# An attention block between two int8 feed-forward blocks on one core: score steps regrouped into nine full-PSUM cycles, with a new hand-placed order

## Chip, core and metric

The kernel runs on one core of a Trainium2 chip. The metric is the device time of one execution in microseconds; 2193.93 us is the median of three runs before the change (2192.86 to 2195.85). Five engines work side by side, each through its own list of instructions in the order in which the program issues them: TensorE (PE in the profile, its weight loads PEld), VectorE (DVE), ScalarE (ACT), GpSimd (POOL) and SyncE (SP), which here issues every DMA. TensorE writes only to PSUM, which has eight banks of 128 partitions by 512 float32; a result must be read out by ScalarE or VectorE before its bank can be written again.

## The reference, cut to what matters

```python
def ffn(lhs, rhs):                                   # int8 feed-forward, rhs 512x512
    lhs_scale = max(absmax(lhs, axis=2), 1e-12) / 127
    rhs_scale = max(absmax(rhs, axis=0), 1e-12) / 127
    acc = int8(round(lhs / lhs_scale)) @ int8(round(rhs / rhs_scale))
    return acc * lhs_scale * rhs_scale

def attn(x, Wk, Wq, Wv, Wo, bo, ...):                # 16 heads of 32
    k, q, v = x @ Wk.T, x @ Wq.T, x @ Wv.T
    k, q = layernorm_per_head(k, kln_g, kln_b), layernorm_per_head(q, qln_g, qln_b)
    dot = causal(einsum('bihd,bjhd->bhij', q * s, k * s))
    return einsum('bhij,bjhd->bihd', softmax(dot), v) @ Wo.T + bo

x = x + 0.5 * ffn(layernorm(x), rhs)                 # x is (8, 1024, 512) float32
x = x + attn(layernorm(x), ...)
x = x + 0.5 * ffn(layernorm(x), rhs)
```

## The kernel before

**Units.** There are 8 batches of 1024 tokens and 16 heads. The work is cut into 32 units; a unit is one batch and a group of four heads (`Unit`, L1220). Tokens go in tiles of 128, eight to a batch. All matrix products of the attention are float32; the two feed-forward products are bf16.

**What a unit does.** For each token tile `project` (L1231 to L1240) makes q, k and v of the four heads: four products over the 512 inputs, 384 columns wide, in two halves. `take` copies them out of PSUM on ScalarE (a square, a copy of q and k, a copy of v). `squares`, `logs`, `newton` and `divide` normalise q and k over a pair of tiles; `block`, `send` and `fetch` transpose them through DRAM; `gain` applies the learned scale. Then the scores are made twice. `m_scores` (L1367) makes them with queries on the partitions, and `m_max` (L1386 and L1392) reduces them on VectorE to each query's negative maximum; `m_both`, `m_turn` and `m_wide` (L1405 to L1423) send it through DRAM so that `m_shift` (L1435) subtracts it from q. `e_scores` (L1447) then makes the shifted scores with keys on the partitions, `e_exp` (L1467) takes the exponential on ScalarE into a tile `pt`, GpSimd zeroes the part above the diagonal (L1471) and adds `pt` tiles up for the denominators (`e_add`, L1488). `e_sum` (L1498) multiplies `pt` with v into `p_o`; `e_out` copies it out; `e_den` (L1516), `e_fold`, `e_rec`, `e_wide` and `e_mult` turn the sums of `pt` into reciprocals and multiply.

**Tiling of TensorE.** A score product has only 32 rows (one head), so four of them run at once in the four row groups of the array: rows of the profile marked 32*128. `e_sum` and `e_den` have 32 columns per head and run four at once in column groups (128*32). Everything else uses the whole array (128*128).

**Steps.** A unit has nine score tiles of 512 columns for the maxima (`MTILES`) and nine for the exponentials (`ETILES`), each for two pairs of heads. `fill` (L1579) issues one tile of one head pair of each kind: four heads side by side. So a unit has 18 steps. The pair of heads that runs in the maximum differs from the one in the exponential, and the two kinds are of neighbouring units, shifted by two steps.

**PSUM before.** `ps_m` and `ps_e` are two banks each, one buffer each: every step writes both, and the next step can't start until `m_max` and `e_exp` have read them. `ps_p` (two buffers of a bank) serves `project` and the output product, `ps_x` (one bank) the feed-forward products, `e_den` and transposes, and `p_o` (one bank) is open over the ten sums of `SUMS`, three for the first half of the queries and seven for the second.

**Feed-forward and output.** `First` (L1110) does the first feed-forward of one token tile and the layer norm ahead of the attention; `Last` (L1169) multiplies a token tile's attention output with Wo (`project`, L1184 and L1186, four products and a bias), adds x and does the second feed-forward. Each unit carries two tiles of each. `Norm` (L996) takes statistics on VectorE, makes `ve`, `rstd` and `off` on GpSimd and applies them on ScalarE. The attention output stays in SBUF (`oT`, ten buffers of 128x512).

**Order.** No scheduler runs: every piece of work has a place, a number in steps, in one of the tables `PLACES` (for units 0 to 29), `BEGIN` and `END`. The pieces are sorted by unit times 18 plus place, and issued in that order; that is the order on every engine and of the DMAs on SP. Waits come from the data alone.

Of the kernel before, what the change touches and what calls it, by code (L numbers as in the profile page):

```python
# [15 lines left out]
P = 128  # L16
# [8 lines left out]
STEPS = 18  # L25
ROWS = 12
COLS = 6
SKEW = 2

# [14 lines left out]
SUMS = [(0, [0]), (1, [0, 1]), (2, [0]), (3, [0]), (2, [1]), (4, [0]), (5, [0]), (6, [0]), (7, [0])]  # L44
SUMS.append((8, [0, 1]))
FIRST_SUMS = (0, 3)
LAST_SUMS = (2, 9)
# [12 lines left out]


PLACES = {
    ('sum', 0): 5.76,
    ('add', 0, 0): 16.945,
    ('add', 0, 1): -44.756,
    ('sum', 1): 8.25,
    ('add', 1, 0): 6.75,
    ('add', 1, 1): 8.69,
    ('sum', 2): 8.4,
    ('add', 2, 0): 8.114,  # L70
    ('add', 2, 1): 10.315,
    ('sum', 3): 11.425,
    ('add', 3, 0): 25.206,
    ('add', 3, 1): -4.272,
    ('sum', 4): 11.495,
    ('add', 4, 0): 12.483,
    ('add', 4, 1): 11.717,
    ('sum', 5): 12.804,
    ('add', 5, 0): 12.935,
    ('add', 5, 1): 12.5,  # L80
    ('sum', 6): 18.244,
    ('add', 6, 0): 15.9,
    ('add', 6, 1): 13.525,
    ('sum', 7): 18.31,
    ('add', 7, 0): 17.065,
    ('add', 7, 1): 15.19,
    ('sum', 8): 18.465,
    ('add', 8, 0): 20.55,
    ('add', 8, 1): 18.625,
    ('sum', 9): 19.911,  # L90
    ('add', 9, 0): 20.96,
    ('add', 9, 1): 21.25,
    ('out', 0): 10.283,
    ('out', 1): 20.235,
    ('den', 0): 12.75,
    ('fold', 0): 13.375,
    ('rec', 0): 18.5,
    ('wide', 0): 19.625,
    ('mult', 0): 23.125,
    ('den', 1): 23.38,  # L100
    ('fold', 1): 24.636,
    ('rec', 1): 26.25,
    ('wide', 1): 26.489,
    ('mult', 1): 29.251,
    ('m', 'both'): 17.25,
    ('m', 'wide'): 18.19,
    ('m', 'turn'): 17.81,
    ('shift', 0): 19.451,
    ('shift', 1): 22.71,
    ('project', 0, 0): 1.5,  # L110
    ('project', 0, 1): 1.911,
    ('take', 0): 2.424,
    ('project', 1, 0): 2.288,
    ('project', 1, 1): 2.625,
    ('take', 1): 2.636,
    ('project', 2, 0): 3.625,
    ('project', 2, 1): 4.125,
    ('take', 2): 5.05,
    ('project', 3, 0): 4.375,
    ('project', 3, 1): 6.375,  # L120
    ('take', 3): 7.125,
    ('project', 4, 0): 7.935,
    ('project', 4, 1): 9.255,
    ('take', 4): 9.625,
    ('project', 5, 0): 9.81,
    ('project', 5, 1): 10.56,
    ('take', 5): 12.25,
    ('project', 6, 0): 13.425,
    ('project', 6, 1): 14.875,
    ('take', 6): 15.875,  # L130
    ('project', 7, 0): 15.864,
    ('project', 7, 1): 16.25,
    ('take', 7): 16.44,
    ('squares', 0): 3.756,
    ('logs', 0): 3.786,
    ('divide', 0): 6.25,
    ('squares', 1): 7.315,
    ('logs', 1): 8.27,
    ('divide', 1): 10.69,
    ('squares', 2): 12.668,  # L140
    ('logs', 2): 13.25,
    ('divide', 2): 15.739,
    ('squares', 3): 17.864,
    ('logs', 3): 18.636,
    ('divide', 3): 19.853,
    ('block', 0): 6.625,
    ('block', 1): 12.19,
    ('block', 2): 16.745,
    ('block', 3): 19.96,
    ('first', 0): {'load': -7.904, 'begin': -4.565, 'root': 1.125, 'norm': 3.114, 'scale': 4.489, 'round': 6.06, 'whole': 7.9, 'flip': 8.201, 'product': 10.429, 'add': 10.5, 'store': 11.125, 'root2': 13.31, 'norm2': 18.375, 'block': 18.5, 'send': 22.25},  # L150
    ('last', 0): {'load': 6.125, 'low': 7.125, 'high': 7.25, 'begin': 7.765, 'root': 8.5, 'norm': 9.0, 'scale': 9.685, 'round': 11.625, 'whole': 11.9, 'flip': 11.972, 'product': 16.065, 'add': 17.865, 'store': 30.9},
    ('first', 1): {'load': -25.875, 'begin': 7.375, 'root': 8.272, 'norm': 11.75, 'scale': 14.86, 'round': 16.38, 'whole': 18.494, 'flip': 19.9, 'product': 21.125, 'add': 22.625, 'store': 24.62, 'root2': 25.076, 'norm2': 26.625, 'block': 27.125, 'send': 29.125},
    ('last', 1): {'load': 15.05, 'low': 17.625, 'high': 19.3, 'begin': 19.375, 'root': 19.386, 'norm': 20.011, 'scale': 20.96, 'round': 22.185, 'whole': 23.69, 'flip': 24.054, 'product': 26.75, 'add': 27.25, 'store': 52.125},
    ('newton', 0): 4.96,
    ('newton', 1): 9.424,
    ('newton', 2): 13.375,
    ('newton', 3): 19.05,
    ('send', 0): 8.199,
    ('fetch', 0): 8.701,
    ('gain', 0): 10.815,  # L160
    ('send', 1): 12.549,
    ('fetch', 1): 15.875,
    ('gain', 1): 17.75,
    ('send', 2): 17.646,
    ('fetch', 2): 18.315,
    ('gain', 2): 19.9,
    ('send', 3): 20.25,
    ('fetch', 3): 20.565,
    ('gain', 3): 24.136,
    ('bring', 0): -4.825,  # L170
    ('bring', 1): -2.81,
    ('bring', 2): -0.386,
# [629 lines left out]
def macaron_kernel(  # L802
# [179 lines left out]
    def rhs_row(c):  # L982
# [3 lines left out]
        if c == NK - 1:  # L986
            nc.vector.tensor_copy(rs_bc, p_rs)
# [815 lines left out]
```

## Time and profile before

| | |
|---|---|
| median of three runs | 2193.93 us |
| span of the profiled execution | 2191.2 us |
| VectorE, ScalarE, GpSimd busy | 1722.6, 1380.5, 1816.7 us |
| instructions | 40293 |
| DMA | 268.01 MB, 49.7% of 16 engines' span |
| `p_qkv` products (L1240) | 709.4 us in 1920 records |
| score products, 512 columns (L1367, L1447) | 434.6 and 430.1 us in 1536 records each |
| adds of `pt` on GpSimd (L1488) | 1071.6 us in 620 |
| exponentials of 1024 columns (L1467) | 586.9 us in 576, mean 1020 ns |
| maxima of 1024 columns (L1386) | 312.5 us in 256, mean 1221 ns |

A float32 product appears as two records, so 1920 records of `p_qkv` are 960 products. A record's duration contains the time in which it overlaps its neighbours, so on TensorE the distance between starts says more than the durations. `nmT` (L1412) is written once in a unit and marks the units: 25 of them start between 429.9 and 1961.5 us, which is 63.82 us for each; the five between 183.9 and 429.9 us, which carry no second feed-forward yet, are 61.5 us apart.

### The profile page before, as it was taken

How to read it: one execution, taken by the hardware profiler on the slowest of the kernel's cores; microseconds unless marked ns; L12 is line 12 of the kernel's file. 1: busy time of each engine (PE TensorE's matmuls, PEld its weight loads, DVE VectorE, ACT ScalarE, POOL GpSimd, SP SyncE). 2: the span in 40 equal slices, each digit the busy share in tenths (PEclk: the TensorE clock that was granted, in tenths of full speed). 3: DMA queues.
4: the chain of work that ended last, by engine and by line, in shares of the span. 5: the costliest groups of instructions: out<-in, count | busy, mean ns of one | idle time of the engine just before them, and what ended most of it. 6: DMA issues, size and time to landing. Idle time of an engine off the chain costs nothing. (4 is left out here: it accounts for less than half of the span.)

```text
span 2191.2 us, 40293 instructions
## 1 busy us (share of the span) xinstructions
PE 2089.8 (95%) x12881; PEld 927.6 (42%) x13000; DVE 1722.6 (79%) x4029; ACT 1380.5 (63%) x2719; POOL 1816.7 (83%) x2376
## 2 busy tenths in 40 slices
PE   5899999999999999999999999999999999999887
PEld 2444443444444444444444444444444444444332
DVE  7677777888888888888878888888888877776776
ACT  5556666666666666666666666666666666556454
POOL 5348898888999898899889889888989888887665
PEclk9999999999999999999999999999999999999998
DMA  6234554555555555555555555555555554443221
GB/s 192 68 104 117 119 126 119 129 132 118 128 134 133 142 138 139 120 130 133 131 141 143 135 121 130 133 132 141 143 137 114 125 126 110 122 113 87 64 60 64
DMA packets 715318, 268.01 MB, mean 122 GB/s; under 512 B 472673, under 2 KB 669281, under 8 KB 715106
## 3 DMA queue, kind: packets, MB, share of 16 engines
q1 hardware_dynamic: 715106, 265.43, 49.7%
q8 instruction: 103, 1.69, 0.3%
q14 instruction: 109, 0.89, 0.1%
HBM read 166.22 MB, written 82.82 MB: 114 GB/s over the span
## 5 line engine op out<-in xcount | busy, mean ns | idle before, releaser
L1488 POOL TENSOR_TENSOR pt<-pt,pt 128x768 f32<-128x768 f32 (+1 forms) x620 | 1071.6, 1736 | 52.2 <-PE p_o L1498 25.1
L1467 ACT ACTIVATE pt<-p_t 128x1024 f32<-128x1024 f32 x576 | 586.9, 1020 | 523.3 <-PE p_t L1447 485.6
L1240 PE MATMUL p_qkv<-wall,yT 128*128 128x384 f32 x1920 | 709.4, 500 | 0.0
L1367 PE MATMUL p_s<-qk 32*128 32x512 f32 (+3 forms) x3072 | 657.3, 523 | 32.3 <-DVE nm L1392 22.3
L1392 DVE CUSTOM_DVE_ANT_0 p_s<-p_s,masks 128x128 f32<-128x128 f32 (+3 forms) x1024 | 511.1, 499 | 223.9 <-PE p_t L1447 171.9
L1447 PE MATMUL p_t<-qk 32*128 32x512 f32 (+3 forms) x3072 | 647.1, 524 | 6.2 <-DVE qk L1435 4.5
L1240 PEld LDWEIGHTS p_qkv<-wall,yT 128*128 128x128 f32 x1920 | 343.4, 189 | 310.6 <-issue 122.0
L1386 DVE TENSOR_REDUCE nm<-p_s 128x2 f32<-128x1024 f32 x256 | 312.5, 1221 | 118.2 <-PE p_t L1447 107.1
L1367 PEld LDWEIGHTS p_s<-qk 32*128 32x128 f32 x3072 | 228.7, 184 | 379.1 <-issue 189.4
L1471 POOL TENSOR_SCALAR_AFFINE_SELECT pt<-pt 128x256 f32<-128x256 f32 x512 | 230.2, 471 | 107.3 <-ACT pt L1467 103.8
L1498 PE MATMUL p_o<-pt,v 128*32 128x512 f32 (+3 forms) x3072 | 293.4, 497 | 1.1 <-ACT oU L1509 1.1
L1447 PEld LDWEIGHTS p_t<-qk 32*128 32x128 f32 x3072 | 245.2, 185 | 49.1 <-issue 10.8
L1186 PE MATMUL p_w_b<-wo,oT 128*128 128x512 f32 x496 | 231.0, 598 | 4.5 <-issue 4.5
L1350 ACT ACTIVATE qk<-qk,qk_b,qk_g 128x256 f32<-128x256 f32 x240 | 130.2, 591 | 108.8 <-DMA qk<-qkd 108.8
L1498 PEld LDWEIGHTS p_o<-pt,v 128*32 128x32 f32 x3072 | 86.8, 110 | 193.6 <-issue 141.4
L1392 DVE DVE_READ_ACCUMULATOR2_ANT nm<- 128x1 f32 x1024 | 144.6, 141 | 0.0
L1186 PEld LDWEIGHTS p_w_b<-wo,oT 128*128 128x128 f32 x496 | 92.5, 191 | 82.2 <-issue 76.6
L1257 ACT ACTIVATE sq<-p_qkv 128x256 f32<-128x256 f32 x256 | 98.2, 384 | 34.9 <-PE p_qkv L1240 34.9
L1106 POOL TENSOR_TENSOR f_a<-f_a,xin_a 128x512 f32<-128x512 f32 x64 | 91.0, 1423 | 32.0 <-DVE f_a L1103 15.8
L1292 DVE TENSOR_TENSOR c<-c,hr 128x512 f32<-128x512 f32 x128 | 112.2, 877 | 4.0 <-ACT yT_a L1144 2.1
L1260 ACT COPY c<-p_qkv 128x256 f32<-128x256 f32 x256 | 96.7, 378 | 0.0
L1268 DVE TENSOR_REDUCE hss<-sq 128x16 f32<-128x512 f32 x128 | 84.6, 661 | 7.1 <-ACT sq L1257 7.1
(124 smaller groups left out, 2231.2 us busy)
## 6 DMA issues: line engine op xcount, KB each, us to landing
yT<-yd_a SPq DMA_DIRECT2D x240, 256.0 KB, 3.1
qkd<-cT SPq DMA_DIRECT2D x480, 64.0 KB, 2.0
qk<-qkd SPq DMA_DIRECT2D x120, 256.0 KB, 3.6
xin_a<-in_x_dram SPq DMA_DIRECT2D x64, 256.0 KB, 4.6
x1d_a<-f_a SPq DMA_DIRECT2D x64, 256.0 KB, 3.1
nmw<-nmd SPq DMA_DIRECT2D x128, 128.0 KB, 2.8
x1r_b<-x1d_a SPq DMA_DIRECT2D x64, 256.0 KB, 3.1
out_dram<-f_b SPq DMA_DIRECT2D x64, 256.0 KB, 2.3
```

What stands on the lines that cost most here:

```text
L1186: nc.tensor.matmul(self.p_w, oT[self.b, g, hf][:, o : o + P], wo[:, g, :], start=False, stop=(g == groups[-1] and len(groups) > 2 or g == ...
L1240: nc.tensor.matmul(self.p[:, : 3 * P], self.yT[t][:, kc, :], wall[:, kc, self.g].rearrange("p a f -> p (a f)"), start=(kc == 0), stop=(kc ...
L1292: nc.vector.tensor_tensor(c, c, self.r.unsqueeze(2).to_broadcast([P, 16, HD]), ALU.mult)
L1350: nc.scalar.activation(part, part, AF.Identity, scale=qk_g[:, a : a + 1], bias=qk_b[:, a : a + 1])
L1367: nc.tensor.matmul(self.pm[:, hh, c0 : c0 + n].rearrange("p (t i) -> p t i", i=P), self.rows(0, h, it * P, P)[:, 0], self.rows(1, h, ch * ...
L1386: nc.vector.tensor_reduce(nm[:, hs], self.pm[:, :, c0 : c0 + n], AX.X, ALU.max, negate=True)
L1392: nc.vector.tensor_tensor_reduce(out=self.pm[:, hh, c0 : c0 + n], in0=self.pm[:, hh, c0 : c0 + n], in1=masks[:, HALF - n :], scale=-1.0, s ...
L1447: nc.tensor.matmul(self.pes[pr][:, hh, c0 : c0 + n].rearrange("p (t i) -> p t i", i=P), self.rows(1, h, jt * P, P)[:, 0], self.rows(0, h, ...
L1467: nc.scalar.activation(pt, self.pes[pr], AF.Exp, scale=scale)
L1471: nc.gpsimd.affine_select(out=pt[:, :, c0 : c0 + P], in_=pt[:, :, c0 : c0 + P], compare_op=ALU.is_ge, fill=0.0, base=0, pattern=[[0, 2], [ ...
L1488: eng.tensor_tensor(acc, acc, self.pt[i, pr][:, :, c0 : c0 + n], ALU.add)
L1498: nc.tensor.matmul(self.p_o[h * HD : (h + 1) * HD, o : o + n], self.v[:, jt, h * HD : (h + 1) * HD], self.pt[i, h // 2][:, h % 2, c0 : c0 ...
```

## The change

The names are kept; the order, the PSUM and the size of the pieces are new.

- A unit has 9 cycles instead of 18 steps. `row` issues both head pairs of a tile one after the other: slot 0 writes banks 0 to 3 (exponential scores of pair 0 in 0 and 1, maximum scores of pair 1 in 2 and 3), slot 1 banks 4 to 7 (pair 1 and pair 0). `e_exp`, the masks and `m_max` are pieces of their own with their own places. For pair 0 the exponential is two instructions of 512 columns, one for each bank (`SPLIT`). The exponentials run one cycle behind.
- PSUM is one tile of eight banks. Projections, sums, denominators and feed-forward products write into banks of a row after these have been read; `SLOTS` names the bank of each.
- `project` makes a token tile's four products in one piece. The sums are three pieces instead of ten; the second half of the queries is summed in two of them, and VectorE adds the two (`e_out`).
- q and k are normalised, transposed and sent in groups of four token tiles instead of two. `First` and `Last` take two token tiles at a time: the sums, `rstd`, `scale`, `whole`, `add`, `block` and the DMAs are one instruction for both, while `bn_stats`, `norm`, `round` and the products stay single. `bring` loads two tiles.
- `off` moves from GpSimd to VectorE; `hsc` (half the token's scale) goes, since the half is folded into `rs_bc`.
- `e_add` writes the second half's accumulator into a tile of its own (`acc`); `pt` has ten buffers instead of eight and four.
- The attention output goes to DRAM: `e_store` writes a half unit's `oT` (256 KB), `Last.heads` loads four groups of heads for two token tiles (512 KB). At the end, the last batch's tiles load three groups and take the fourth from SBUF.
- The places of all pieces, `BEGIN` and `END` among them, are new numbers.

```diff
-STEPS = 18
-SKEW = 2
+CYCLES = 9
-SUMS = [(0, [0]), (1, [0, 1]), (2, [0]), (3, [0]), (2, [1]), (4, [0]), (5, [0]), (6, [0]), (7, [0])]
-SUMS.append((8, [0, 1]))
+SUMS = [
+    [(0, 0), (1, 0), (1, 1), (2, 0)],
+    [(3, 0), (4, 0), (5, 0), (2, 1)],
+    [(6, 0), (7, 0), (8, 0), (8, 1)],
+]
+SLOTS = {
+    ('project', 0): 7,
+    ('project', 1): 0,
+    ('project', 2): 4,
+    ('project', 3): 2,
...
+    ('sum', 2): 4,
...
+banks = psum.tile([P, 8, HALF], F32, name="banks")
...
-    def fill(eu, mu, es, ms):
...
+    def row(eu, ei, mu, mi):
+        for slot in range(2):
+            for sub in range(2):
+                if mu is not None:
+                    mu.m_scores(mi, slot, sub)
+                if eu is not None:
+                    eu.e_scores(ei, slot, sub, 4 * slot)
...
         def e_exp(self, i, pr):
...
+            if pr in SPLIT:
+                for hh in range(2):
+                    nc.scalar.activation(pt[:, hh], pe[:, hh], AF.Exp, scale=scale)
...
+        def e_out(self, s):
+            p_o = self.p_o.pop(s)
+            if s == 2:
+                nc.vector.tensor_tensor(self.oU[1], p_o, self.oU[1], ALU.add)
+                return
...
+        def off(self):
+            self.shift = small.tile([P, self.n], F32, tag="off", name=f"off_{self.tag}", bufs=6)
+            nc.vector.scalar_tensor_tensor(
+                self.shift, self.mv[:, :, 0], -1.0, self.rstd, ALU.mult, ALU.mult
+            )
...
+        def heads(self):
+            g = self.groups
+            self.o = self.tile([P, g, self.n * P], F32, "o")
+            t0 = self.ts[0]
+            nc.sync.dma_start(
+                out=self.o,
+                in_=od[self.b][: g * P, t0 * P : (t0 + self.n) * P].rearrange("(g p) t -> p g t", p=P),
+            )
...
+        def begin(self, j):
+            nc.vector.tensor_tensor(self.x1[:, j], self.p_w[j], self.x1[:, j], ALU.add)
+            self.begun += 1
+            if self.begun == self.n and self.groups == NG:
+                self.stats(self.x1)
...
+        def e_store(self, hf):
...
+            nc.sync.dma_start(
+                out=od[self.b][self.g * P : (self.g + 1) * P, hf * HALF : (hf + 1) * HALF],
+                in_=oT[self.u, hf],
+            )
```

In a steady unit the new table gives TensorE this order by cycle (W is the output product of a token tile, F a feed-forward product, Q a projection, S a sum, D a denominator): 0: row, W, S2; 1: row, Q1, Q0; 2: row, Q3, Q2, F; 3: row, F, Q4, S0; 4: row, Q5, D1; 5: row, Q7, Q6; 6: row, D0, S1; 7: row alone; 8: row, F, F, W. VectorE's order from row 0 to row 2 is: maxima of slot 1, a reciprocal, maxima of slot 0, `shift`, `begin` with the statistics of two tiles, `e_out` of S2, the statistics of `First`, `off`; then maxima of slot 1, `scale` of `Last`, maxima of slot 0.

## Prediction, made before the changed kernel was run

> **What bounds the kernel now.** I read the busy times by stage first (two single units, 63.8 and 63.6 us), then TensorE's own order of time inside a unit, then the order of time of all engines around two score steps. The columns of the first view are the stretch, its length, busy us of PE, PEld, DVE, ACT and POOL with counts, granted clock, DMA share, GB/s.
>
> ```profile
> 590.00:653.80 63.80, 63.21 (x400) 28.11 (x403) 52.86 (x124) 42.47 (x84) 56.99 (x76) 1.00 0.56 133
> 1197.30:1260.90 63.60, 63.01 (x403) 28.16 (x406) 53.09 (x126) 42.49 (x85) 57.71 (x76) 1.00 0.56 134
> ```
>
> TensorE is busy 99% of a unit at clock 1.00, GpSimd 90%, VectorE 83%. The reader should not take 99% for full use, since a busy row ends where the next begins. What TensorE loses is seen in the distances between starts:
>
> ```profile
> 1011.30 1.45 PE L1240 MATMUL p_qkv<-wall,yT 128*128 128x384 f32 x4
> 1012.69 1.07 PE L1498 MATMUL p_o<-pt,v 128*32 128x384 f32 x16
> ...
> 1023.56 2.85 PE L1240 MATMUL p_qkv<-wall,yT 128*128 128x384 f32 x8
> 1026.34 0.70 PE L1367 MATMUL p_s<-qk 32*128 32x512 f32 x2
> ...
> 1052.79 1.06 PE L1516 MATMUL p_d<-pt,ones 128*32 128x512 f32 x8
> 1053.67 1.04 PE L1498 MATMUL p_o<-pt,v 128*32 128x512 f32 x8
> 1054.64 0.70 PE L1367 MATMUL p_s<-qk 32*128 32x512 f32 x2
> ...
> 1055.71 1.56 PE L1240 MATMUL p_qkv<-wall,yT 128*128 128x384 f32 x4
> ...
> 1058.27 1.56 PE L1240 MATMUL p_qkv<-wall,yT 128*128 128x384 f32 x4
> 1059.76 0.70 PE L1367 MATMUL p_s<-qk 32*128 32x512 f32 x2
> ```
>
> Four records of a projection ahead of scores take 1.49 us (1058.27 to 1059.76), eight take 2.78: a record streams 0.32, and 0.20 is left for the change of the array's tiling. A record of 512 columns streams 0.43 by the same rate, so eight in four-way tiling (two rounds) need 0.86. `p_d` ahead of `p_o`, the same tiling, takes 0.88: no change, no loss. `p_o` ahead of scores takes 0.97 (0.11 lost), a score step ahead of a projection 1.07 (0.21 to 0.22 lost), a projection ahead of `p_o` 1.39 (0.10 lost). The 18 steps bring 36 changes, other neighbours three more: 39 times about 0.20 is 7.8 us of the 63.8. The remaining 56.0 us is streaming, and I see no wait in it: the kernel is bound by TensorE, an eighth of it changes of tiling.
>
> **The change, part by part.** *Rows instead of steps, whole projections, three sums.* The streaming is the same work. By the order in the text of the change, 9 rows have 8 exits (row 7 runs into row 8): 8 x 0.22 = 1.76. They are entered twice from projections (0.20 each), four times from sums or denominators (0.11) and twice from W or F, for which I take the 0.11 of the nearest row: 1.06. Three projections or W go into column tiling: 0.30. Sum 3.1, against 7.8: 4.7 us less, a unit of 59.1 if TensorE never waits. Between slot 0 and slot 1 the tiling stays, so by the row of `p_d` nothing is lost there; bounds 0 and 9 x 0.22 = 2.0.
>
> *The waits that this brings.* A row takes all banks, so whatever follows waits for a reader of that same row. The delays:
>
> ```profile
> 1049.79 1.23 DVE L1386 TENSOR_REDUCE nm<-p_s 128x2 f32<-128x1024 f32 x1 [0.85 <-PE p_t L1447]
> 1051.11 0.30 PEld L1367 LDWEIGHTS p_s<-qk 32*128 32x128 f32 x4 [0.41 <-DVE nm L1386]
> ...
> 1055.82 1.23 DVE L1386 TENSOR_REDUCE nm<-p_s 128x2 f32<-128x1024 f32 x1 [0.32 <-PE p_t L1447]
> 1055.87 1.02 ACT L1467 ACTIVATE pt<-p_t 128x1024 f32<-128x1024 f32 x1 [0.18 <-PE p_t L1447]
> ```
>
> The scores that began at 1054.64 are read 1.18 us later by VectorE and 1.23 by ScalarE; a reader that ends at 1051.02 lets TensorE go at 1051.11, 0.09 later. A row streams 1.72, the change included it is left at 1.94. So I walk through a unit. *Cycle 7* has a row and nothing else: row 8's slot 0 starts at 1.18 + 1.23 + 0.09 = 2.50 instead of 1.72, a wait of 0.78; its slot 1 waits for the second maximum (started 1.14 after the first, as the next instruction at 1031.59 was after a start at 1030.45), 0.3 more: 1.1. *Cycle 2*: Q3 goes into bank 2, which the masked maxima of slot 0 read: 0.79 and 0.70 for two heads (L1392 at 512 columns): 1.18 + 0.79 + 0.70 + 0.09 = 2.76 against 1.94: 0.8. *Cycle 6*: D0 in bank 1 waits for two half exponentials, each as the 0.58 copy of 512 columns (L1509): 1.23 + 1.16 + 0.09 = 2.48 against 1.94: 0.5. *Cycles 0 and 1* are VectorE's: from 2.04 (slot 1's scores) it has four sets of masked maxima of 1.93 (1005.80 to 1007.73, 1016.42 to 1018.35), reciprocal 0.25, `shift` 0.79, `begin` 0.72 and two tiles' statistics 1.8, S2's add 0.72, statistics 1.8, `off` 0.2, `scale` 1.2 + 0.3: 15.5, so row 2's banks 2 and 3 are free at 17.6. TensorE comes there after 1.72 + 3.65 + 2.56 + 1.72 + 5.16 streamed and 0.85 of changes, 15.7: 1.9. Cycles 3, 4, 5 and 8 come out at 0 to 0.3 each; I take 0. Together 4.3 of the 4.7 come back: 63.4 against 63.82. Bounds: nothing waits (59.1), or each of the other four cycles also waits 0.3 and the slots lose 2.0 (66.6).
>
> *ScalarE*: the split costs 9 x (2 x 0.58 - 1.02) = 1.3 a unit; `logs` halves, 8 x 0.26 = 2.1 less; covered by 21 us of idle time, except where an exponential stands behind `norm` or `round` (2 x 0.80) in its queue, as in cycles 1 and 3. *GpSimd*: `off` 1.7, `hsc` 1.3, half of `rstd` and `ve` (0.57 and 0.22 to 0.35 each, three less) about 2, half of `newton` 1.5, so 57 falls to about 50.5: its sums of `pt` keep their price. Not on the path; uncovered it would be worth 0. *VectorE*: S2's add and `off` come, half of the 0.15 and 0.16 of `scale` goes: 53 stays 53, of a shorter unit.
>
> *DMA.* The output's round trip adds 256 KB x 2 written and 512 KB read a unit: 1 MB to 8.5 MB, at the 134 GB/s of the unit 8 us more of transfers, on a DMA share of 0.56. The nearest row, a 256 KB load, lands in 3.1. `heads` is issued after row 8, and the last half unit's `e_store` comes in cycle 7; W1 needs it two cycles later. SP loses issues (8 loads of q, k, v input become 4, 16 `send` become 8): priced at 0, bounds -0.3 and +3.1 once a batch, 25 us in all if the store is late for it.
>
> *Start and end.* The start lasts to 183.9, the end from 2026 to 2191. Steps and sums are joined there too, some 30 changes x 0.2 = 6 us; bounds 15 either way, from the 349 us being less than two thirds streaming.
>
> The sum against the profiled execution: 29 unit distances x -0.42 = -12, and -6, so 2173 in place of the span of 2191.2. The median of the runs lies 2.7 above that span: **2176**.
>
> A rule that speaks against the change: the Trainium skill, TensorEngine Tiling (Array Packing), section PSUM Bottleneck, says that tiling speeds up TensorE but not the reading of PSUM, which may become the bottleneck. If reading bounded the whole unit, VectorE's 53 us would be below TensorE's 59.1 and nothing would come back; the walk says it does cycle by cycle. The same skill, SBUF, section Who interferes with whom, says a VectorE instruction with two SBUF inputs contends with GpSimd's reads; the product on L1292 took 679 ns at the least, 682 in the median and 2008 at the most, which agrees, and was free while VectorE had 11 us to spare.
>
> **Rivals.** *The banks come free early.* Cycles 0 and 1 wait only where VectorE is late at row 0; if its list is ahead, 1.9 and part of cycle 2 go, and a unit is 59.1 + 1.9 = 61: 2194 - 29 x 2.8 - 6 = 2107. For it: VectorE idles 11 us a unit now. Against: S2's add stands behind the statistics in its list. *VectorE decides.* One mechanism: in cycles 0 and 1 its 15.5 us leave no slack, so each delay of a `begin`, an `off` (it waits for GpSimd's `rstd`) or an instruction with two SBUF inputs delays a row, and rows delay its next maxima. From 4.7 us of waits on it is a loss; with the product's mean of 896 instead of 682 ns and the same 0.2 for some ten such instructions it is 63.4 + 2 = 65.4: 2194 + 29 x 1.6 - 6 = 2234. Against: the other cycles give VectorE time to catch up. *The gain is as good as given back*: waits of 4.6 to 4.8, start and end even, 2194 within 0.2%. That a row's readers serialise because all banks are one tile is excluded by nothing in the trace of before; it would look like the second rival and cost more.
>
> **Chances.** Forecast (2150 to 2189) 0.45; early banks (2060 to 2150) 0.20; no difference 0.09; VectorE decides (2198 to 2270) 0.26. The measurement can tell about 0.2%, 4.4 us. Faster 0.65, same 0.09, slower 0.26. The range leaves out half of the early banks and two fifths of the slow case: 2095 to 2226. The forecast's own range is 2150 to 2189.
>
> **What would show it.** The distance of `nmT` from unit to unit: 63.4; 61 or 65.4 for the rivals. Starts within a row: slot 1 0.86 after slot 0 and no loss between them; each loss of 0.1 to 0.22 only at 19 places. Waits of TensorE for maxima in cycles 1, 2 and 7, for exponentials in cycle 6. VectorE without idle time from row 0 to row 2. I am wrong if TensorE waits on GpSimd's masks, on a DMA, or on ScalarE's queue instead, or if start and end move by more than 15.

## The result: slower by 4.7%

2298.65 us (median of 4 runs, 2293.28 to 2301.09) against 2194.89 us: ratio 1.0465, 95% interval 1.0447 to 1.0483. The profiled span grew from 2191.2 to 2291.6 us. By the marks of `nmT`, one a unit, the start up to the first mark is 13.5 us shorter, the end from the last mark 3.5 longer, the first five units 3 longer, the last 3.6 shorter, and the 25 units between are 68.2 instead of 63.8 us each: 111 us. So the loss lies in the steady unit.

The busy times of two units of the changed kernel; columns: stretch, length, busy us of PE, PEld, DVE, ACT and POOL with counts, clock, DMA share, GB/s:

```profile
1034.49:1101.80 67.31, 62.15 (x400) 30.27 (x402) 51.33 (x117) 40.26 (x79) 50.16 (x51) 1.00 0.56 138
1101.80:1169.00 67.20, 62.54 (x400) 30.46 (x402) 50.61 (x116) 40.25 (x79) 49.49 (x51) 1.00 0.58 139
```

Before, TensorE lacked 0.6 us of a unit; now it lacks 5, at the same clock in these units. Over the steady part the granted clock stood at 0.5 in four stretches, 17 us together, which costs some 8 of the 111 us; before it never did. GpSimd fell from 57 to 50, as predicted, and VectorE from 53 to 51, where 53 had been predicted. The idle time of TensorE, in its own order of time (start, busy us, what it does, in brackets the wait and who ended it):

```profile
1029.23 0.70 PE L1637 MATMUL banks<-qk 32*128 32x512 f32 x2 [0.99 <-DVE nm L1656]
...
1033.18 0.38 PE L1464 MATMUL banks<-bo,ones_bf 128*128 128x512 bf16 x1
1035.13 3.70 PE L1466 MATMUL banks<-wo,o_b 128*128 128x512 f32 x8 [1.57 <-DMA o_b<-od]
...
1049.31 0.70 PE L1710 MATMUL banks<-qk 32*128 32x512 f32 x2 [0.53 <-DVE oU L1775]
...
1053.67 2.85 PE L1514 MATMUL banks<-wall,yT 128*128 128x384 f32 x8 [0.45 <-DVE nm L1660]
1057.22 1.07 PE L1637 MATMUL banks<-qk 32*128 32x512 f32 x2 [0.70 <-DVE nm L1660]
```

Row 8 waits for maxima, as foreseen. W's first product waits for a load from DRAM, which had been priced at nothing. Then row 1, Q0 and row 2 wait for VectorE. VectorE's own order of time shows what kept it, and SP's (the queue that issues all DMAs) what kept that:

```profile
1034.49 0.21 DVE L1678 STREAM_TRANSPOSE nmT<-nm 128x32 f32<-128x32 f32 x1
...
1045.66 0.80 DVE L1698 SCALAR_TENSOR_TENSOR qk<-nmw,qk 128x512 f32<-128x512 f32 x1 [1.58 <-DMA nmw<-nmd]
...
1050.79 1.28 DVE L1270 SCALAR_TENSOR_TENSOR off_fb<-mv_fb,rstd_fb 128x2 f32<-128x2 f32 x1
...
1054.91 0.90 DVE L1319 TENSOR_SCALAR sc_b<-amax_b 128x2 f32<-128x2 f32 x1
```

```profile
1029.09 0.46 SPq L1457 DMA_DIRECT2D o_b<-od  x1
...
1031.49 5.51 SPq L1607 DMA_DIRECT2D qkd<-cT  x4
1037.10 2.11 SPq L1681 DMA_DIRECT2D nmd<-nmT  x4
...
1040.34 1.70 SPq L1688 DMA_DIRECT2D nmw<-nmd  x4
```

The attention output's load is issued at 1029.09 and read at 1035.13. The maxima leave VectorE at 1034.70, go to DRAM and back (`nmd`, `nmw`), and the shift that needs them starts 11 us later; `oU` (which empties the bank that row 1's slot 1 needs, at 1048.59) and the statistics stand behind it. Two instructions on 256 numbers take 1.28 and 0.90 us. Over the steady part (430 to 1950 us, 23 units) the view of waits gives for the changed kernel (us in total, times, longest):

```profile
DVE qk L1698 <- DMA nmw<-nmd: 50.0, 23, 3.8
PEld banks L1466 <- DMA o_b<-od: 47.9, 22, 3.0
```

and for the kernel before, where nothing waited for an attention output and the shift for almost nothing:

```profile
DVE qk L1435 <- DMA nmw<-nmd: 0.8, 2, 0.6
```

The same way of the maxima in the kernel before, VectorE and SP:

```profile
1004.48 0.21 DVE L1412 STREAM_TRANSPOSE nmT<-nm 128x32 f32<-128x32 f32 x1
...
1013.15 0.69 DVE L1435 SCALAR_TENSOR_TENSOR qk<-nmw,qk 128x512 f32<-128x512 f32 x1
```

```profile
1004.72 1.79 SPq L1415 DMA_DIRECT2D nmd<-nmT  x4
1007.57 1.69 SPq L1423 DMA_DIRECT2D nmw<-nmd  x4
```

There the shift came 8.46 us after `nmT` had ended (1004.69 to 1013.15) and waited for nothing: the maxima were back by then. In the changed kernel its turn was no earlier, 9.38 us after `nmT` (1045.66 less the wait of 1.58, from 1034.70), but the way took longer. The store was issued 2.4 us after `nmT`, behind the four issues of `send` 1, and the transfers took longer to land, in the median over the steady part:

```profile
nmw<-nmd SPq DMA_DIRECT2D x92, 128.0 KB, 2.8
```

before, and in the changed kernel:

```profile
nmw<-nmd SPq DMA_DIRECT2D x92, 128.0 KB, 4.2
```

The stores `nmd` took 2.2 instead of 1.7. No run tests why the transfers take longer to land.

### The profile page after: what moved, and what is told of

Read it like the earlier page. It is cut to its first block, busy times and chain, and to the rows that moved or that the text cites. A ratio compares the mean times of both kernels' runs of the same rounds, so it can differ in the third digit from the quotient of the medians.

```text
span 2291.6 us, 38090 instructions
## 1 busy us (share of the span) xinstructions
PE 2063.5 (90%) x12923; PEld 1003.5 (44%) x12984; DVE 1706.7 (74%) x3789; ACT 1311.2 (57%) x2571; POOL 1589.5 (69%) x1640
## 4 chain that ended last, share of the span: by engine, by line
PE 46%; DVE 18%; SPq 13%; DMA 10%; ACT 5%; POOL 4%; issue 3%; DVEq 0%; POOLq 0%; another core or an unknown queue 0%; ACTq 0%
PE banks L1514 23%; PE banks L1637 8%; SPq L1607 7%; PE banks L1710 6%; DMA nmw<-nmd 5%; PE banks L1761 4%; PE banks L1783 3%; DMA nmd<-nmT 2%; PE banks L1350 2%; POOL acc L1754 2%; SPq L1681 2%; DVE c L1565 2%; ACT y_b L1276 2%; DVE st_fb L1258 2%; SPq L1688 2%
## 5 line engine op out<-in xcount | busy, mean ns | idle before, releaser
L1754 POOL TENSOR_TENSOR acc<-acc,pt 128x512 f32<-128x512 f32 (+1 forms) x372 | 699.3, 1886 | 5.3
L1514 PE MATMUL banks<-wall,yT 128*128 128x384 f32 x1920 | 665.4, 495 | 12.1 <-DVE nm L1660 10.6
L1637 PE MATMUL banks<-qk 32*128 32x512 f32 (+3 forms) x3072 | 615.5, 515 | 64.5 <-DVE nm L1656 32.1
L1710 PE MATMUL banks<-qk 32*128 32x512 f32 (+3 forms) x3072 | 595.5, 521 | 32.7 <-DVE oU L1775 15.3
L1660 DVE CUSTOM_DVE_ANT_0 banks<-banks,masks 128x128 f32<-128x128 f32 (+3 forms) x1024 | 469.9, 522 | 142.6 <-PE banks L1710 83.5
L1725 ACT ACTIVATE pt<-banks 128x512 f32<-128x512 f32 x576 | 312.4, 596 | 317.2 <-PE banks L1710 263.8
L1514 PEld LDWEIGHTS banks<-wall,yT 128*128 128x128 f32 x1920 | 353.6, 190 | 306.8 <-ACT pt L1725 46.5
L1637 PEld LDWEIGHTS banks<-qk 32*128 32x128 f32 x3072 | 252.1, 188 | 268.4 <-DVE nm L1656 91.0
L1656 DVE TENSOR_REDUCE nm<-banks 128x2 f32<-128x1024 f32 x256 | 304.4, 1210 | 25.5 <-PE banks L1637 13.8
L1710 PEld LDWEIGHTS banks<-qk 32*128 32x128 f32 x3072 | 273.1, 189 | 111.2 <-issue 32.7
L1727 ACT ACTIVATE pt<-banks 128x1024 f32<-128x1024 f32 x288 | 294.6, 1024 | 11.0 <-PE banks L1710 5.8
L1754 POOL TENSOR_TENSOR pt<-pt,pt 128x768 f32<-128x768 f32 (+1 forms) x186 | 235.0, 1277 | 6.4 <-PE banks L1761 1.4
```

The source lines that it names most:

```text
L1514: nc.tensor.matmul(p[:, : 3 * P], self.yT[t][:, kc, :], wall[:, kc, self.g].rearrange("p a f -> p (a f)"), start=(kc == 0), stop=(kc == NK ...
L1637: nc.tensor.matmul(self.pm[i, slot][:, hh, c0 : c0 + n].rearrange("p (t i) -> p t i", i=P), self.rows(0, h, it * P, P)[:, 0], self.rows(1, ...
L1656: nc.vector.tensor_reduce(nm[:, hs], pm[:, :, c0 : c0 + n], AX.X, ALU.max, negate=True)
L1660: nc.vector.tensor_tensor_reduce(out=pm[:, hh, c0 : c0 + n], in0=pm[:, hh, c0 : c0 + n], in1=masks[:, HALF - n :], scale=-1.0, scalar=-NEG ...
L1710: nc.tensor.matmul(self.pes[i, pr][:, hh, c0 : c0 + n].rearrange("p (t i) -> p t i", i=P), self.rows(1, h, jt * P, P)[:, 0], self.rows(0, ...
L1725: nc.scalar.activation(pt[:, hh], pe[:, hh], AF.Exp, scale=scale)
```

## Experiments

For every run I give the median, the ratio to the kernel before with its interval, and the loss of TensorE at the places that differ: from the first start of a group of matmuls to the first start of the next, less what the group streams, mean over the steady units. W0 is the output product in cycle 8, W1 the one in cycle 0. The change of tiling alone is about 0.13 at W0, 0.30 at row 1, 0.24 at Q1 and Q0, 0.34 at row 2 and 0.24 at rows 7 and 8; the rest is wait. "Unit" is the mean distance of `nmT` over 25 units. The losses contain time at a lower granted clock. Between 430 and 1950 us it stood at 0.5 for 17 us in the changed kernel, 31 in heads_early, narrow and narrow_heads, 44 in both_divide, 48 in both_stats, 51 in send_split, 89 in half_logs, 92 in half_stats and 133 in best1, for none in both, half2 and half2n, and for 10 or less in the others. Half of such a time is lost, and no run tests what sets it off.

| run | W0 | row 1 | Q1, Q0 | row 2 | rows 7, 8 | unit |
|---|---|---|---|---|---|---|
| the change | 2.52 | 2.22 | 1.79 | 0.59 | 1.78 | 68.20 |
| heads_early | 0.70 | 3.07 | 1.79 | 0.55 | 1.78 | 67.21 |
| const_shift | 2.30 | 1.45 | 1.73 | 0.61 | 1.78 | 67.04 |
| both | 0.60 | 0.89 | 1.65 | 0.61 | 1.78 | 64.88 |
| s2_copy | 2.20 | 0.91 | 3.06 | 0.61 | 1.78 | 67.83 |
| half_turn | 0.13 | 0.31 | 1.86 | 0.61 | 1.78 | 66.17 |
| half_shift | 0.17 | 0.30 | 1.39 | 0.61 | 1.78 | 65.47 |
| half2 | 0.76 | 0.30 | 1.20 | 0.61 | 1.86 | 64.07 |
| narrow | 2.98 | 2.03 | 0.24 | 0.34 | 1.78 | 66.56 |
| half2n | 0.70 | 0.30 | 0.24 | 0.34 | 1.88 | 62.70 |

### Two waits, one at a time

**heads_early** issues the attention output's load just behind the store that it reads.

```diff
-    ('last', 'heads'): 8.4794,
+    ('last', 'heads'): 7.775,
```

> Only the load of the attention output from DRAM (heads) is issued earlier on SP, just behind the store that it reads, ahead of the fold of the sums. In the changed kernel W's first product waits about 2.4 us per unit for that load. Theory (the waits add up): most of that wait goes and stays gone, 1.3 to 2.4 us in each of some 31 units, so 2225 to 2260 us against 2299. Rival (the waits only move: VectorE's list in cycles 0 and 1, or the maxima's way through DRAM, is the limit): W starts earlier but row 1 of slot 1 and Q wait the longer, 2285 to 2305 us.

2269.24 us, 1.0346 (1.0320 to 1.0372): 30 us, less than the theory's 40 to 75. W0's wait went, but VectorE's wait for the maxima rose from 50.0 to 67.9 us and row 1 took 0.85 back. Both had a part.

**const_shift** takes VectorE's wait away (the edit puts the constant into both halves of the shift).

```diff
         def m_shift(self, hf):
...
-            m = self.nmw[:, hf * HALF : (hf + 1) * HALF].rearrange("p (t i) -> p t i", i=P)
+            m = ones.unsqueeze(1).to_broadcast([P, NT // 2, P])
```

> The shift of the first half's scores reads a constant in place of the maxima that came back from DRAM; so the maxima are left out of the result. The transfers stay, only VectorE's wait for them (1.6 us per unit, 50 us in the steady part) goes. Theory: VectorE begins its list of cycles 0 and 1 that much earlier and row 1 of slot 1 (2.0 us of wait) and Q and row 2 (1.6 us) wait 1.6 to 2.5 us less per unit: 2220 to 2250 us. Rival (W's wait for the attention output then ends the same cycle, or the list's own length decides): under 0.5 us per unit, 2283 to 2300 us.

2256.89 us, 1.0293 (1.0275 to 1.0311): 42 us, just short of the theory's range. Row 1 gained; Q and row 2 didn't, which was a first sign that something else held them.

**both** has the two edits.

> The two edits together: early load of the attention output, constant in the shift (maxima left out of the result). Theory (two separate waits, in W and ahead of row 1): their gains add, 3 to 4.9 us per unit, 2145 to 2205 us. Rival (one wait behind the other, they share what they cover): no better than the better one of the two by more than 0.5 us per unit, 2215 us or more.

2201.14 us, 1.0026 (1.0006 to 1.0045): 97 us, more than 30 and 42 together. Two chains lie side by side until row 1: TensorE's through W0, VectorE's through the shift. Shortening one alone runs into the other, so each single run understated its wait.

**s2_copy** takes the addition of `oU` off VectorE.

```diff
-                nc.vector.tensor_tensor(self.oU[1], p_o, self.oU[1], ALU.add)
+                nc.scalar.copy(self.oU[1], p_o)
```

> The addition that empties the sums' bank of the second half moves from VectorE to a copy on ScalarE; the addition of the first part of that sum is left out. Theory (row 1 of slot 1 waits for VectorE's queue, not for the bank as such): that row's wait of 2.0 us falls below 0.7 and VectorE's list is 0.7 us shorter ahead of Q: 1.0 to 2.0 us per unit, 2237 to 2268 us. Rival (what row 1 gains, Q and row 2 wait the longer, since VectorE still begins late): under 0.7 us per unit, 2277 to 2300 us.

2284.53 us, 1.0427 (1.0392 to 1.0463): the rival. Row 1 lost 0.91 instead of 2.22, and Q took 1.27 of the 1.31: VectorE was late as a whole, not this one addition.

### Reordering that failed, and what it showed

**both_stats** and **both_divide** move work of VectorE in the kernel of both.

```diff
-    ('first', 'stats2'): 9.9305,
+    ('first', 'stats2'): 10.87,
...
-    ('first', 'off2'): 10.9483,
+    ('first', 'off2'): 11.14,
```

> The kernel of both (early load of the attention output, constant in the shift, maxima left out of the result) with one more edit: the layernorm statistics of First's rows go on VectorE from ahead of the maxima of cycle 1 to behind them. In both (2201 us) the projections Q1 and Q0 behind row 1 lose 1.65 us per unit. Theory (VectorE's list in cycle 1, not the banks as such, holds them): that loss falls to 0.5 to 0.9, so 0.7 to 1.2 us per unit, 2163 to 2180 us. Rival (Q waits for row 1's own maxima however the list stands, or the statistics are then late for First): under 0.3 us per unit or slower, 2192 to 2215 us.

2277.03 us, 1.0387 (1.0369 to 1.0406). Q1 and Q0 did gain 0.72, but `off2` was now late for ScalarE's `ay`, which waited 3.24 for it at 1052.00 with an exponential behind it, and Q3 waited for that exponential: 3.75 instead of 0.36. The edit moved two things, so it did not test the theory.

```diff
-    ('divide', 1): 6.9483,
+    ('divide', 1): 7.1275,
```

> The kernel of both (maxima left out of the result) with VectorE's second divide, which waits 1.0 us for GpSimd, moved behind the maxima of row 7's slot 0. In both the rows 7 and 8 lose 1.78 us per unit, of which 1.1 had been predicted. Theory (the divide ahead of the maxima costs the rest): 0.4 to 0.7 us per unit, 2178 to 2190 us. Rival (row 8 waits for row 7's own maxima alone, or the later divide makes block 1, send 1 and fetch 1 late): no gain, 2195 to 2215 us.

2268.57 us, 1.0353 (1.0335 to 1.0370), a miss in both theories' terms: the divide, 1.91 us long, now stood between the two maxima of row 7, and rows 7 and 8 lost 3.37 instead of 1.78.

**send_split** gives ScalarE two of the four issues of `send` 1.

```diff
-                nc.sync.dma_start(out=to[:, :, w, :], in_=self.cT[hf][w * W : (w + 1) * W])
+                (nc.scalar if hf and w > 1 else nc.sync).dma_start(
+                    out=to[:, :, w, :], in_=self.cT[hf][w * W : (w + 1) * W]
+                )
```

> Nothing is left out. The early load of the attention output, and two of the four DMAs of send 1 are issued by ScalarE in place of SP, where all four hold up the maxima's store nmd for 2.6 us. Theory (VectorE waits for the maxima because their two transfers stand behind send 1 on SP): the maxima land 2.0 to 2.8 us sooner and most of what the constant in the shift gave (68 us between the two runs) comes without it: 2200 to 2235 us. Rival (the transfers, not SP's queue, take the time, or ScalarE's issues delay gain 0 and the exponentials by as much): 2255 to 2280 us.

2263.35 us, 1.0333 (1.0315 to 1.0350): the rival, 6 us below heads_early, and the two intervals overlap. It spent 20 us more at the clock of 0.5, which hides some 10 us of a gain. SP's order of time in this run:

```profile
1023.78 2.23 SPq L1683 DMA_DIRECT2D nmd<-nmT  x4
...
1028.54 1.69 SPq L1690 DMA_DIRECT2D nmw<-nmd  x4
```

and VectorE's:

```profile
1023.54 0.21 DVE L1680 STREAM_TRANSPOSE nmT<-nm 128x32 f32<-128x32 f32 x1
...
1033.76 1.21 DVE L1700 SCALAR_TENSOR_TENSOR qk<-nmw,qk 128x512 f32<-128x512 f32 x1 [2.10 <-DMA nmw<-nmd]
```

Now `nmd` goes out the moment the maxima are there, and the shift still starts 10.0 us after `nmT` ended: two issues of 2.2 and 1.7 us and two landings. So the place on SP is not what keeps it long here: with SP free the way is still 1.5 us longer than the 8.46 that were enough before. **best1** put the three on top of each other:

> Nothing is left out: send_split with the statistics behind the maxima and the divide behind the maxima of row 7's slot 0. Theory (these waits add): 1.1 to 1.9 us per unit below send_split, 2150 to 2200 us, at or below the kernel before (2193). Rival (VectorE's work in cycles 0 and 1 decides whatever its order): no more than 0.4 us per unit below send_split, over 2205 us.

2380.39 us, 1.0861 (1.0833 to 1.0889): Q3 lost 4.29 and rows 7 and 8 3.93, the two misplacements added up, with 133 us at the clock of 0.5 on top.

### Sending half of the maxima early

The maxima of the first 512 tokens are complete after row 2, and the shift ahead of row 1 needs only these. **half_turn** sends them by a transpose and eight DMAs of their own.

```diff
+    ('m', 'early'): 2.8461,
+    ('m', 'half'): 3.7,
...
+        def m_early(self):
+            nmT = small.tile([P, W], F32, tag="nmT", name=f"nmE_{self.u}", bufs=2)
+            nc.vector.transpose(
+                nmT.rearrange("p (h o t) -> p h o t", h=NG, o=2),
+                self.nm[:, :, : NT // 2].unsqueeze(2).to_broadcast([P, NG, 2, NT // 2]),
+            )
...
```

> Nothing is left out. Early load of the attention output, and the maxima of the first half of the tokens, which are complete after row 2, go through DRAM in cycles 2 to 4 by a transpose and eight DMAs of their own; the shift stays where it is and the second half goes as before. Theory (row 1 waits for the maxima's way through DRAM, about 10 us from row 8's last maxima, which no reordering of SP's queue shortens): the wait of VectorE ahead of the shift (68 us in the steady part of heads_early) goes to zero and the time falls from 2269 to that of both, 2195 to 2215 us. Rival (eight more DMAs and a transpose per unit cost SP and VectorE as much, or the wait is taken by gain 0): 2240 us or more.

2235.26 us, 1.0182 (1.0164 to 1.0200). The wait ahead of the shift is gone and row 1 loses nothing but its change of tiling, 0.31. The time lies between the theory and the rival. 34 us are missing to both: S0, the sum in cycle 3, lost 0.93 instead of 0.16 and row 5 1.61 instead of 0.25. **half_shift** moves the shift too.

```diff
-    ('shift', 0): 9.667,
+    ('shift', 0): 5.9535,
```

> half_turn with the shift of the first half moved from cycle 0, ahead of row 1, to cycle 5 of the cycle before, where VectorE idles about 2 us ahead of the sums of squares. Theory (VectorE's list of cycles 0 and 1 holds row 1, Q and row 2): 0.76 to 1.4 us less in that list, 0.3 to 1.0 us per unit: 2165 to 2200 us. Rival (the bank of row 1 slot 1 and the list's other members decide; the shift only moves): within 8 us of half_turn.

2208.68 us, 1.0069 (1.0048 to 1.0090). Q1 and Q0 gained 0.47 and a unit 0.70, as the theory had it, but S0 and row 5 stayed as bad and the time is 9 us above its range. **half_stats** repeats the move of the statistics alone, **half_logs** adds one on ScalarE:

```diff
-    ('first', 'stats2'): 9.9305,
+    ('first', 'stats2'): 10.53,
```

> half_shift with the layernorm statistics of First moved behind the maxima of slot 1 in cycle 1 only (both_stats had put them, and the offset that needs them, two steps further, and Q3 then waited). Theory: Q0 waits 0.7 to 1.4 us less per unit and nothing else is late, 2135 to 2175 us. Rival (as in both_stats: the layernorm is late and holds Q3 or row 3): slower than half_shift.

> half_stats with ScalarE's four small operations of the second q/k norm ahead of the copy of the denominators in cycle 6, so that GpSimd and VectorE's second divide, which waits 1.0 us there, come earlier. Theory (the divide ahead of the maxima of row 7 delays row 8): 0.2 to 0.6 us per unit, 6 to 18 us below half_stats. Rival (row 8 waits for row 7's own maxima): within 4 us of half_stats.

2292.19 us, 1.0448 (1.0422 to 1.0473), and 2285.12, 1.0412 (1.0392 to 1.0432). half_logs took rows 7 and 8 from 1.81 to 1.25, and the two intervals overlap. half_stats is a miss by over 100 us, and the most useful one: slower than half_shift, as the rival had it, but Q1 and Q0 lost 4.03 and row 2 2.08, not Q3. VectorE in this run:

```profile
1048.60 2.30 DVE L1272 SCALAR_TENSOR_TENSOR off_fb<-mv_fb,rstd_fb 128x2 f32<-128x2 f32 x1 [0.20 <-POOL rstd_fb L1268]
...
1055.14 2.25 DVE L1321 TENSOR_SCALAR sc_b<-amax_b 128x2 f32<-128x2 f32 x1
```

and GpSimd:

```profile
1048.54 2.35 POOL L1779 TENSOR_TENSOR acc<-acc,pt 128x1024 f32<-128x1024 f32 x1
...
1055.03 4.11 POOL L1779 TENSOR_TENSOR acc<-acc,pt 128x1024 f32<-128x1024 f32 x2
```

Two instructions on 128x2 last as long as the GpSimd addition that began just before: 1048.60 + 2.30 = 1050.90, and the addition ends at 1048.54 + 2.35 = 1050.89. They do not compute for 2.3 us, they wait inside. With the statistics moved, they met the addition at its start instead of in its middle (1.28 and 0.90 in the changed kernel), and TensorE's row 2 waited 3.44 us at 1058.79. Behind that wait the clock fell as well (0.55 over the stretch; columns as above):

```profile
1058.79:1062.60 3.81, 3.81 (x24) 3.01 (x24) 2.28 (x9) 3.46 (x7) 0.34 (x1) 0.55 0.15 34
```

So some 46 of the miss are TensorE at half its clock, and not the waits themselves.

### The lock between VectorE and GpSimd

**narrow** changes the form of the offsets and scales, and nothing else of the changed kernel. Each becomes two instructions of one column, and the offset, which read two tensors, now reads one tensor and one number per partition.

```diff
-            nc.vector.scalar_tensor_tensor(
-                self.shift, self.mv[:, :, 0], -1.0, self.rstd, ALU.mult, ALU.mult
-            )
+            for j in range(self.n):
+                nc.vector.tensor_scalar(
+                    self.shift[:, j : j + 1], self.mv[:, j, 0:1], self.rstd[:, j : j + 1], -1.0, ALU.mult, ALU.mult
+                )
...
-            nc.vector.tensor_scalar(self.sc, amax, 1e-12, 1.0 / INT8_MAX, ALU.max, ALU.mult)
+            for j in range(n):
+                nc.vector.tensor_scalar(
+                    self.sc[:, j : j + 1], amax[:, j : j + 1], 1e-12, 1.0 / INT8_MAX, ALU.max, ALU.mult
+                )
```

> The changed kernel, nothing else moved: the offset and the scale of the token pairs are computed column by column (two 128x1 instructions with one tensor input each) instead of one 128x2 instruction. Theory (a 128x2 instruction waits inside for GpSimd's running addition, a 128x1 with one tensor input doesn't): offset and scale take 0.15 each, no maximum over 0.3, VectorE's list ahead of Q0 and row 2 is 1.5 us shorter, 0.5 to 1.5 us per unit: 2250 to 2284 us. Rival (the durations are only waits for the operand, or Q and row 2 wait for something else): the durations stay or the time does, 2292 to 2305 us.

2251.68 us, 1.0254 (1.0234 to 1.0275): 47 us. The edit touches all three offsets and both scales of a unit, but only the two above had been long: `off_fa`, `off_l` and `sc_a` took 169, 148 and 169 ns in the median in the changed kernel, in the same 128x2 forms. The groups of one instruction (count, shortest/median/longest in ns) in the kernel before, the changed kernel and narrow:

```profile
L1066 DVE TENSOR_SCALAR sc_b<-amax_b x48: 153/154/156, 444.5 to 1939.5; 128x1 f32<-128x1 f32 x48
```

```profile
L1319 DVE TENSOR_SCALAR sc_b<-amax_b x23: 904/912/1621, 442.5 to 1938.7; 128x2 f32<-128x2 f32 x23
```

```profile
L1321 DVE TENSOR_SCALAR sc_b<-amax_b x46: 142/150/154, 437.4 to 1902.7; 128x1 f32<-128x1 f32 x46
```

The offset of the same rows: 1262 to 2291 ns in the changed kernel, 180 to 214 each in narrow. Q1, Q0 and row 2 lose nothing but the change of tiling, 0.24 and 0.34. Of the 28 `sc_b` of 128x2 in the changed kernel every one ended 23 to 29 ns after the addition during which it had begun. So the wait at Q and row 2 was this lock: making the blocks pairwise had turned a scale that GpSimd's additions never touched into one that waits for them, and the offset, which had been on GpSimd, came to VectorE in a form that does. For the offset the two tensors matter and not the width. Near the end of the changed kernel, where it still has one column, it met an addition that ran from 2252.68 for 1.81 us, and ended with it:

```profile
2253.27 1.25 DVE L1270 SCALAR_TENSOR_TENSOR off_fb<-mv_fb,rstd_fb 128x1 f32<-128x1 f32 x1
```

The Trainium skill, VectorE: DVE Perf Modes, section What auto-detection actually checks, says that a single-source instruction with source and destination in SBUF takes a two-port mode when the outermost dimensions longer than one element are even in both, or equal. The same skill, SBUF — State Buffer, section Who interferes with whom, says that such an instruction contends with GpSimd for a shared port pair, that one with two SBUF inputs contends with a GpSimd instruction that reads SBUF, and that whichever issues first has the pair for the whole instruction. The trace agrees: the scale waits with 2 columns and not with 1, the offset with two tensors waits with either, and the wait ends with the addition.

### Whether the waits add up

**half2** is half_shift with the early DMAs at other places on SP:

```diff
-    ('m', 'early'): 2.8461,
-    ('m', 'half'): 3.7,
+    ('m', 'early'): 3.195,
+    ('m', 'half'): 4.35,
```

since in half_shift SP had been held by a load of `xin`, and TensorE waited for the load behind it:

```profile
1043.97 0.39 SPq L1378 DMA_DIRECT2D xin_a<-in_x_dram  x1
1044.47 0.42 SPq L1510 DMA_DIRECT2D yT<-yd  x1
```

```profile
1049.24 5.40 PE L1516 MATMUL banks<-wall,yT 128*128 128x384 f32 x16 [1.02 <-DMA yT<-yd]
```

> half_shift with the early transpose and its four DMAs behind First's send on SP and the broadcast load behind the load of x's input: in half_shift the send and, behind a load that waits, a projection's input came late (1.0 us of TensorE's wait for yT ahead of Q5, 0.7 ahead of S1). Theory (SP's order): both go, 1.0 to 2.2 us per unit: 2140 to 2178 us. Rival (the eight more transfers as such, or VectorE's place): within 8 us of half_shift, 2200 to 2217 us.

2175.53 us, 0.9912 (0.9895 to 0.9928): S0 (which the expectation calls S1) and row 5 are back at 0.16 and 0.26. **half2n** adds narrow, **half2nl** the move of half_logs:

> half2 with narrow's edit. Theory (the lock holds Q and row 2): 0.5 to 1.2 us per unit below half2, 2105 to 2160 us, below the kernel before and within what had been forecast for the change. Rival: within 6 us of half2.

> half2n with ScalarE's four small operations of the second q/k norm ahead of the copy of the denominators in cycle 6 (half_logs: rows 7 and 8 lost 1.25 instead of 1.80). Theory: 0.4 to 0.6 us per unit below half2n, 12 to 18 us. Rival (another wait takes it, as in half_logs, 7 us): 0 to 8 us.

2136.70 us, 0.9738 (0.9723 to 0.9752), and 2136.91, 0.9733 (0.9710 to 0.9756). half2n beats both kernels and leaves nothing out. half2nl gained 0.62 at rows 7 and 8 and lost most of it at W0 (1.14 instead of 0.70), and its unit is no shorter: the rival. Two units of half2n, same columns as above:

```profile
974.60:1036.77 62.17, 60.76 (x403) 30.21 (x402) 49.87 (x122) 40.38 (x79) 50.30 (x51) 1.00 0.58 146
1036.77:1099.99 63.22, 60.79 (x403) 30.17 (x402) 49.83 (x121) 40.39 (x79) 50.25 (x51) 1.00 0.61 153
```

Its VectorE, and TensorE, whose Q1 and Q0 now run without a break until row 2 at 992.85:

```profile
987.91 0.30 DVE L1273 TENSOR_SCALAR off_fb<-mv_fb,rstd_fb 128x1 f32<-128x1 f32 x2
...
990.93 0.21 DVE L1323 TENSOR_SCALAR sc_b<-amax_b 128x1 f32<-128x1 f32 x2
```

```profile
987.49 5.43 PE L1520 MATMUL banks<-wall,yT 128*128 128x384 f32 x16
```

**late_heads** and **narrow_heads** put one wait back into half2n: the late load of the attention output, or the late way of the maxima.

> half2n with the load of the attention output back at its place behind row 8: the one wait of W0 alone, nothing else of the changed kernel's waits left. Theory (the wait of 2.2 to 2.4 us per unit is worth its full length where no other wait follows it): 1.8 to 2.4 us per unit above half2n, 2190 to 2215 us. Rival (rows 0 and 1 catch up, as they did in the changed kernel, where the early load gave 1.0 us per unit): 2155 to 2175 us.

> The changed kernel with narrow's edit and the early load, the maxima's way through DRAM as in the changed kernel: the wait of VectorE ahead of the shift alone. Theory (row 1 then loses about 3 us per unit to the maxima's way, all of it on TensorE's path): 2.0 to 2.9 us per unit above half2n, 2200 to 2228 us. Rival (the early load's gain adds in full to narrow's, 2252 less 60 or more): under 2192 us.

2172.71 us, 0.9912 (0.9893 to 0.9932): a unit of 64.07, 1.37 more, in the rival's range; W0 loses 2.29, but the 0.70 that half2n loses there is not new. 2226.32 us, 1.0161 (1.0122 to 1.0200): 65.65, 2.95 more, as the theory had it. The lock is half2 less half2n, 1.37. From half2n, 62.70 + 1.37 + 2.95 + 1.37 = 68.39, and the changed kernel's unit is 68.20: the three account for the difference within 0.2. The 2.95 is not the wait alone. half2n also moves the shift itself out of VectorE's list of cycles 0 and 1, which was worth 0.70 from half_turn to half_shift. Taking only the wait away was worth 2.33 from heads_early to both. In both figures about 0.7 is the 31 us at the clock of 0.5 in narrow_heads and in heads_early.

## Why the prediction was wrong, point by point

- **Streaming and changes of tiling: right in kind.** 23 groups of matmuls lose 4.2 us a unit to changes where 3.1 had been worked out (rows 1, 2 and 3, whose pieces are uneven, lose 0.3 each). For before, 7.8 had been worked out. Between the slots nothing is lost, as taken.
- **Cycle 7 (1.1), cycle 6 (0.5), cycle 2 (0.8).** Rows 7 and 8 lose 1.78 less the 0.24 of the change: 1.5. Part of that is the second divide ahead of the maxima; half_logs and half2nl, where it came earlier, lost 1.25. Row 6 loses 0.80 less 0.23: 0.57, right. Row 2 loses nothing ahead of Q3 once the lock is gone; 0.8 was too much.
- **The step that failed first: cycles 0 and 1, "1.9".** In the changed kernel row 1, Q1 and Q0, and row 2 wait 1.92, 1.55 and 0.25 us beyond their changes of tiling, 3.7 in place of 1.9, and W0 adds 2.4 where 0 had been put. The list of VectorE began with the scores of row 0 and priced `shift` at 0.79, as work without a wait. But the shift had to wait for the maxima, 2.33 a unit by heads_early and both. In the trace of before it waited 0.8 us in 23 units, and I took that for no cost. The new order did not bring its turn much nearer to `nmT` (8.46 us before; 9.4 in the unit shown above). It was the way through DRAM that grew, from under 8.5 to about 11 us, and the prediction had no term for that.
- **"`off` 0.2" and "`scale` 1.2 + 0.3" in the same list.** They cost 1.28 and 2.4 (1053.65 to 1056.02: the reduction 1.22, `sc_b` 0.90 instead of 0.15, the reciprocal 0.17): 1.37 a unit on the path. The second rival named this mechanism, an `off` or an instruction with two SBUF inputs that GpSimd delays, and gave it 2.0 a unit and 2234 us. The mechanism was right; that the pairwise 128x2 form brings `scale` into it was not seen, and it was one of three. That the time, 2299, lies near neither this rival's 2234 nor the forecast is due to the other two.
- **The attention output through DRAM, "priced at 0", bound +3.1 a batch.** It is a wait of about 2.4 in W0 every unit, worth 1.37 a unit, not a batch: in the unit shown the load is issued 4.1 us before W's turn (1029.09 and 1033.18), in the median of the steady units 2.9, and such loads land in 4.8 in the median (the nearest row, 3.1, was for half the size). That TensorE would wait on a DMA was named in the prediction as a sign of being wrong. The detour itself is not the cost; half2n has it, with the load issued earlier.
- **The rival of early banks** (61 a unit, 2107) was right about cycles 0 and 1: without the late maxima and the lock, and with the shift moved out of its list, VectorE is in time there. half2n's 62.70 keeps the rest at W0, row 6 and rows 7 and 8.
- **Start and end, -6:** by its bounds (183.9 is the second `nmT`, and 2026 comes just behind the last but one) the start is 9.3 shorter and the end the same.

The forecast's mechanism is in the chip: half2n, the same regrouping with these three places mended, is 58 us faster than the kernel before. What failed is the pricing of two ways through DRAM, the maxima's and the attention output's, and of two small instructions beside GpSimd.

## What to carry to other kernels

When an order and its transfers are regrouped, list every round trip that closes inside it (the maxima out and back, store and load) with its full length from the producer's end to the consumer's start, and compare that with the work left between. A wait of zero in the trace of before says nothing of its slack, and the trip itself can grow when other transfers stand ahead of it. A single experiment on one of two parallel waits shows only the lead that it has over the other. And where GpSimd works beside them, look at the form of small VectorE instructions: here one column and one tensor input stayed free, while two columns or two tensors waited, and one saved instruction of 0.15 us cost up to 2.3.

## What had not been expected of the hardware

- A TENSOR_SCALAR of 128x2 took 904 to 1621 ns beside GpSimd's additions, of 128x1 142 to 154, in the same place of the program. A RECIPROCAL of 128x2 right behind it (`inv_b`) took 165 to 166 in the changed kernel, though most of them began during an addition: not every form of two columns waits.
- `nmT` to `nmw`: 16 KB out and a broadcast of 512 KB back take 10.0 us from the end of the transpose to the shift even when SP is free for it (send_split). The Trainium skill, DMA: Bandwidth & Descriptors, section Anatomy of one DMA — SWDGE (gpsimd) path, gives a fixed cost of about 2 us per DMA, measured on GpSimd's path and not on SP's. Two of those are less than half of what this round trip took.
- Four issues of 128 KB held SP for 5.51 us in the changed kernel (`send` 1, 1031.49), for 4.10 in heads_early (`send` 1, 1025.77) and for 3.07 in send_split (`send` 0, 1009.80): an issue has no fixed price here, and what stands behind it on SP is late by the difference.
- TensorE's granted clock was not the same in all orders: 1.00 all through the steady part of before and half2n, 0.5 for 133 us of best1. In best1, both_stats and half_stats nearly all such stretches came within some 6 us behind a distance of 2.4 to 3.9 us between two starts on TensorE, so that a longer wait was paid for twice; in send_split none did, so the wait is not the only condition.
